# Running the token layers of the first image pair beside the last finish of the scan layers

## The chip, the cores and the metric

The kernel runs on one core of one Trainium2 chip. The metric is the device time of one launch in microseconds. Three runs of the kernel before gave 11881.9 us in the median, from 11853.94 to 11897.37. PE is the matrix engine (PEld its weight loads), DVE the vector engine, ACT the scalar engine, POOL the GpSimd engine, and SP the engine whose queue (SPq) issues the DMAs.

## The reference

Four images of 64x64 positions with 96 channels go through four layers, each with a residual addition.

```python
# layers 0 and 1: group norm, then a selective scan in four directions
x = x + conv_ref(_gn(x), ...)     # projection, 3x3 depthwise conv, SiLU, four scans of 16 states,
                                  # sum of the directions, layer norm, times silu(z), projection
# layers 2 and 3, on tokens: attention without a softmax, then a quantised MLP
t = t + attn_ref(_ln_t(t), ...)   # y = (q k^T) v * scale per head, then a projection
t = t + ffn_ref(_ln_t(t), ...)    # relu(W1 x + b1) in fp8, W2 h + b2
```

The end of a scan layer (the sum of the four directions, the layer norm, the gate `silu(z)`, the projection and the residual) is called the finish here. Layers 2 and 3 are the token layers. Every image is independent of the others in all four layers.

## The kernel before, in words

The images are worked on in pairs. Layers 0 and 1 make four phases: layer 0 on pair 0 and pair 1, then layer 1 on pair 0 and pair 1. Each phase has a preparation (`prepare`), the scan itself (`scan_phase`, whose order is written by hand) and a finish. `Scans.run` runs the preparation of a phase with the finish of the phase before it beside it: both are Python generators, and a number called `beside` says how many finish steps are taken for each preparation step. After the fourth scan, `run` makes one more turn with nothing to prepare, in which the finish of layer 1, pair 1 runs alone. Its result goes to `x2[1]`; the result for pair 0, `x2[0]`, was written a whole phase earlier.

`finish` works in four quarters (L603 to L619 bring one quarter into the layout of tokens, with a matmul by permutations for each direction and a matmul of `ud_f`, and ACT copies of the result) and each quarter in two slices (`finish_slice`: statistics L642, reciprocal root `neg_rsqrt` L115 to L119, normalisation L652 to L657, the gate L669 and L672 with SiLU, product L676, turn back L683, projection L694, residual L696, store L702). A quarter yields 52 times, so the finish has 208 steps.

Then `token_layers` runs. Its pools are opened when the scans' pools are closed. It loads and quantises the weights (L744 to L755, 17 small DMAs on SP, the mask among them), and takes the pairs in turn. For a pair, two generators `image(b)` are stepped in turn: load `t` (L887), for each of two layers `attention` and then the MLP, and store. In both parts the image is cut into eight chunks of 512 tokens, and `side_by_side` keeps two chunks of an image going. So four chains, two for each image, are interleaved. An image has 136 steps: 35 for an attention and 33 for an MLP, twice.

Each chunk begins with a layer norm: a matmul with a matrix of 1/96 gives the mean in a PSUM bank (`mu`, L784), DVE subtracts (L786), ACT squares (L793), a second matmul gives the variance in a second bank (`var`, L797), and `neg_rsqrt` takes Ln (L115), Exp (L116) and Square (L117) on ACT and two DVE operations (L118, L119). L118 reads `var` again, so that bank is held through Ln, Exp and Square. The first chunk of every sweep preloads the activation table that holds both Ln and Exp (L795, 16 times in all). In an MLP three matmuls (L866) are cast by ACT into `h16` (L869), DVE adds and clips (L870) and casts to fp8 (L875), and three matmuls (L878) give `o`.

[...] In the token layers, pool `tp_a` has four for `mu`, `var`, `o` and the small products of the attention, `tp_h` two and `tp_kv` two. In the last finish, the pools `p_c`, `p_d` (for the preparation) and `p_f` (two banks for the finish) are open. Outside of the hand-ordered parts, the framework orders the instructions of each engine out of the program's order and its own idea of what is ready; every engine then runs its own list strictly in order.

Of the kernel before, what the change touches and what calls it, by code (L numbers as in the profile page):

```python
# [9 lines left out]
F32 = mybir.dt.float32  # L10
F16 = mybir.dt.float16
# [4 lines left out]
PSUM = bass.MemoryType.PSUM  # L16
# [3 lines left out]
NP = B // 2  # L20
HW = 64
L = HW * HW
C = 96
# [6 lines left out]
TC = 512  # L30
# [12 lines left out]
NF = HID // 128  # L43
# [69 lines left out]
def neg_rsqrt(nc, cst, var, ln, r, sq):  # L113

    nc.scalar.activation(ln, var, AF.Ln, bias=cst.eps[: var.shape[0]])  # L115
    nc.scalar.activation(r, ln, AF.Exp, scale=-0.5)  # L116
    nc.scalar.activation(sq, r, AF.Square, scale=SQRT_HALF)  # L117
    nc.vector.scalar_tensor_tensor(sq, var, EPS, sq, ALU.add, ALU.mult)  # L118
    nc.vector.scalar_tensor_tensor(r, sq, 1.5, r, ALU.subtract, ALU.mult)  # L119
# [11 lines left out]
class Scans:  # L131
# [11 lines left out]
    def bank(self):  # L143
        return self.p_c.tile([128, TC], F32, name="c")
# [563 lines left out]
    def run(self, phases):  # L708


        for p in range(len(phases) + 1):
            with self.tc.tile_pool(name="p_c", bufs=2, space=PSUM) as self.p_c, self.tc.tile_pool(
                name="p_d", bufs=2, space=PSUM
            ) as self.p_d, self.tc.tile_pool(name="p_f", bufs=2, space=PSUM) as self.p_f:
                end = self.finish(phases[p - 1]) if p > 0 else iter(())
                due = 0.0
                if p < len(phases):
                    for _ in self.prepare(phases[p]):
                        due += phases[p].beside
                        while due >= 1.0:  # L720
                            next(end, None)
                            due -= 1.0
                for _ in end:
                    pass
            if p < len(phases):
                self.scan_phase(phases[p])


@with_exitstack
def token_layers(ctx: ExitStack, tc, cst, a, layers, x_in, x_out):  # L730

    nc = tc.nc
    wp = ctx.enter_context(tc.tile_pool(name="tw", bufs=1))
# [1 line left out]
    raw_p = ctx.enter_context(tc.tile_pool(name="traw", bufs=2))  # L735
    big = ctx.enter_context(tc.tile_pool(name="tbig", bufs=2))
    cp = ctx.enter_context(tc.tile_pool(name="tchunk", bufs=4))
    p_a = ctx.enter_context(tc.tile_pool(name="tp_a", bufs=4, space=PSUM))
    p_h = ctx.enter_context(tc.tile_pool(name="tp_h", bufs=2, space=PSUM))
    p_kv = ctx.enter_context(tc.tile_pool(name="tp_kv", bufs=2, space=PSUM))  # L740

# [29 lines left out]
    def side_by_side(parts, width):  # L771

        parts, active = iter(parts), []
        while True:
            if len(active) < width:
                active += [p for p in (next(parts, None),) if p is not None]
            if not active:
                return
            active = [p for p in active if next(p, p) is not p]
            yield  # L780

    def layernorm(t, cut, out, first, **quant):
        mu = p_a.tile([128, TC], F32, name="pa")
        nc.tensor.matmul(mu[:C], cst.mean_c, t[:, cut], start=True, stop=True)  # L784
        tcn = cp.tile([C, TC], F32, name="tcn")
        nc.vector.tensor_tensor(tcn, mu[:C], t[:, cut], ALU.subtract)  # L786
        yield
        sq = cp.tile([C, TC], F32, name="sq")
        with ExitStack() as order:
            if first:  # L790

                order.enter_context(tc.manual_schedule(engines={mybir.EngineType.Activation}))
            nc.scalar.activation(sq, tcn, AF.Square)  # L793
            if first:
                nc.scalar.preload_act_table_set(LN_EXP)  # L795
        var = p_a.tile([128, TC], F32, name="pa")
        nc.tensor.matmul(var[:C], cst.mean_c, sq, start=True, stop=True)  # L797
        yield
        ln = cp.tile([C, TC], F32, name="ln")
        r = cp.tile([C, TC], F32, name="r")  # L800
        neg_rsqrt(nc, cst, var[:C], ln, r, sq)
        yield
        nc.vector.tensor_tensor(out, tcn, r, ALU.mult, **quant)

# [27 lines left out]
    def attention(t, w):  # L832

        tn = big.tile([C + 1, L], F32, name="tn")
        nc.gpsimd.memset(tn[C : C + 1, :], 1.0)  # L835
        vk_ps = p_kv.tile([C, C], F32, name="vk_ps")
        yield from side_by_side((keys_values(t, tn, vk_ps, w, c) for c in range(NC)), 2)

        vk = cp.tile([C, C], F32, name="vk", bufs=2)
        nc.vector.tensor_tensor(vk, vk_ps, cst.mask, ALU.mult)  # L840
        m_ps = p_a.tile([128, TC], F32, name="pa")[:C, :C]
        nc.tensor.matmul(m_ps, vk, w["ff"], start=True, stop=True)
        m1 = cp.tile([C, C], F32, name="m1", bufs=2)
        nc.vector.tensor_copy(m1, m_ps)
        yield
        m_ps = p_a.tile([128, TC], F32, name="pa")[: C + 1, :C]
        nc.tensor.matmul(m_ps, w["q_t"], m1, start=True, stop=True)
        m2 = cp.tile([C + 1, C], F32, name="m2", bufs=2)
        nc.vector.tensor_copy(m2, m_ps)
        nc.vector.tensor_tensor(m2[C : C + 1], m2[C : C + 1], w["bff"][C : C + 1], ALU.add)  # L850
        yield
        for c in range(NC):
            cut = slice(c * TC, (c + 1) * TC)
            o = p_a.tile([128, TC], F32, name="pa")
            nc.tensor.matmul(o[:C], m2, tn[:, cut], start=True, stop=True)  # L855
            nc.vector.tensor_tensor(t[:, cut], t[:, cut], o[:C], ALU.add)
            yield

    def ffn_chunk(t, w, c):
        cut = slice(c * TC, (c + 1) * TC)  # L860
        xq = cp.tile([C, TC], FP8, name="xq")
        yield from layernorm(t, cut, xq, c == 0, saturate=False)
        h16 = cp.tile([128, NF, TC], F16, name="h16")
        for f in range(NF):
            h_ps = p_h.tile([128, TC], F32, name="ph")
            nc.tensor.matmul(  # L866
                h_ps, w["w1"][:, f * 128 : (f + 1) * 128], xq, start=True, stop=True
            )
            nc.scalar.copy(h16[:, f], h_ps)  # L869
            nc.vector.tensor_scalar(  # L870
                h16[:, f], h16[:, f], w["b1"][:, f : f + 1], 0.0, ALU.add, ALU.max
            )
            yield
        hq = cp.tile([128, NF, TC], FP8, name="hq")
        nc.vector.tensor_copy(hq, h16, saturate=False)  # L875
        o = p_a.tile([128, TC], F32, name="pa")
        for f in range(NF):
            nc.tensor.matmul(o[:C], w["w2"][:, f], hq[:, f], start=f == 0, stop=f == NF - 1)  # L878
        yield
        o16 = cp.tile([C, TC], F16, name="o16")  # L880
        nc.scalar.copy(o16, o[:C])
        nc.vector.tensor_scalar_add(o16, o16, w["b2"])
        nc.vector.tensor_tensor(t[:, cut], t[:, cut], o16, ALU.add)

    def image(b):
        t = big.tile([C, L], F32, name="t")
        nc.sync.dma_start(t.rearrange("c (a p) -> c a p", p=64), x_in[b // 2, :, :, b % 2])  # L887
        for pre in layers:
            yield from attention(t, ws[pre])
            yield from side_by_side((ffn_chunk(t, ws[pre], c) for c in range(NC)), 2)  # L890
        nc.sync.dma_start(x_out[b], t)

    for pair in range(NP):
        both = [image(2 * pair), image(2 * pair + 1)]
        while both:
            both = [i for i in both if next(i, i) is not i]


def body(tc, a, out):
    nc = tc.nc  # L900
    with ExitStack() as ctx:
        cst = Consts(nc, a)
        cst.shared(ctx.enter_context(tc.tile_pool(name="const", bufs=1)))
        dram = ctx.enter_context(tc.tile_pool(name="dram", bufs=1, space=DRAM))
        x1 = dram.tile([NP, C, HW, 2, 64], F32, name="x1")
        x2 = dram.tile([NP, C, HW, 2, 64], F32, name="x2")
        phases = [Phase("L0_", p, a["x"], x1) for p in range(NP)]
        phases += [Phase("L1_", p, x1, x2) for p in range(NP)]
        with ExitStack() as inner:
            Scans(tc, inner, cst, a).run(phases)  # L910
        token_layers(tc, cst, a, ["L2_", "L3_"], x2, out)


def constants():
# [83 lines left out]
```

## Time and profile before

| what | value |
|---|---|
| profiled execution, its own time | 11923.01 us |
| its span, first to last instruction | 11921.2 us (1.8 us lie outside) |
| median of the three runs | 11881.9 us |
| last scan instruction ends, last finish begins | about 10728 us from the span's start |
| last finish ends | about 11055 us |
| pair 0 in the token layers | 11055 to 11482 us, its loads first |
| pair 1 in the token layers | 11482 us to the end |
| busy: PE, DVE, ACT, POOL | 72%, 84%, 62%, 63% of the span |

The span is the time from the first to the last recorded instruction. Busy time of PE is the time in which at least one matmul is under way by the record, with the tail of each matmul in it, so a PE that works in short pieces looks busier than one that works without a break. In the list of stages, each row gives the length of the stretch, the busy time and the instruction count of each engine, the mean granted clock of PE as a share of full speed, the DMA share and the rate.

### The profile page before, as it was taken

The numbers are of one execution on the slowest core, as the hardware profiler recorded it, in microseconds if no ns is written. First come the engines' busy times: TensorE is split into PE (matmuls) and PEld (weight loads), VectorE is DVE, ScalarE is ACT, GpSimd is POOL, SyncE is SP. The second block draws the span as 40 slices with busy tenths as digits, with TensorE's granted clock in tenths as the row PEclk, the third lists the DMA queues.
The fourth block names the chain that finished last, engine by engine and source line by source line (L and its number), as shares of the span: only waits on it lengthen the run. The fifth ranks groups of instructions, "written<-read, shape, count | busy, mean of one in ns | idle before, by whom it ended". The sixth has DMA issues, their size and how long they took to land.

```text
span 11921.2 us, 337611 instructions
## 1 busy us (share of the span) xinstructions
PE 8549.8 (72%) x144992; PEld 4586.7 (38%) x144992; DVE 9991.8 (84%) x10247; ACT 7335.1 (62%) x12106; POOL 7480.2 (63%) x2316
## 2 busy tenths in 40 slices
PE   4557777765767777765767777766667777777777
PEld 1124444432334444442334444433234444444333
DVE  6679999977779999987769999986769999993667
ACT  4556666655556666655556666655557666662556
POOL 0169999961159999970149999980149999980000
PEclk8578999986679999986679999887578898998887
DMA  3677777765677777765777777765677777763110
GB/s 99 192 244 250 253 255 254 251 208 144 201 241 256 253 253 251 253 217 146 204 229 258 256 253 251 253 217 149 198 226 255 255 255 253 253 229 124 18 22 11
DMA packets 952266, 2501.22 MB, mean 210 GB/s; under 512 B 324494, under 2 KB 607220, under 8 KB 819316
## 3 DMA queue, kind: packets, MB, share of 16 engines
q1 hardware_dynamic: 950772, 2479.63, 63.0%
q8 instruction: 1142, 18.71, 0.7%
q14 instruction: 352, 2.88, 0.1%
HBM read 1965.42 MB, written 513.80 MB: 208 GB/s over the span
## 4 chain that ended last, share of the span: by engine, by line
DMA 57%; PE 12%; DVE 11%; SPq 10%; ACT 5%; issue 3%; POOL 2%; POOLq 0%; DVEq 0%; ACTq 0%
DMA h<-du 53%; SPq L408 9%; DVE xc L277 4%; PE f L603 2%; POOL parts L331 2%; PE d L317 1%; DVE dl L328 1%; PE f L683 1%; PE c L300 1%; DVE du_sb L327 1%; PE f L694 1%; DVE parts L332 1%; DMA yk<-y 1%; PE f L669 1%; PE f L612 1%
## 5 line engine op out<-in xcount | busy, mean ns | idle before, releaser
L418 POOL TENSOR_TENSOR h<-h,b 128x1536 f32<-128x1536 f32 x2048 | 7020.9, 3461 | 574.0 <-DMA h<-du 229.6
L435 DVE TENSOR_TENSOR_SCAN h<-a,carry,h 128x512 f32<-128x512 f32 x5376 | 6353.3, 1259 | 202.8 <-POOL h L418 199.4
L428 ACT ACTIVATE a<-a,a_col 128x512 f32<-128x512 f32 x6144 | 4038.5, 664 | 1888.6 <-PE a L424 1852.8
L453 PEld LDWEIGHTS y<-h,cw 128*32 128x32 f32 x131072 | 2785.0, 128 | 3534.2 <-issue 1369.4
L453 PE MATMUL y<-h,cw 128*32 128x48 f32 x131072 | 3658.4, 266 | 522.4 <-DVE h L435 205.3
L424 PE MATMUL a<-dlt,rep 72*128 72x512 bf16 x6144 | 2534.2, 422 | 1352.5 <-DVE h L435 1254.1
L331 POOL CAST parts<-dl 96x1024 bf16<-96x1024 f32 x256 | 431.2, 1688 | 2687.6 <-DVE dl L328 1979.4
L465 ACT COPY d<-y 128x384 f32<-128x384 f32 x2048 | 979.7, 478 | 467.7 <-PE y L453 414.9
L435 DVE TENSOR_TENSOR_SCAN h<-a,h 128x512 f32<-128x512 f32 x768 | 868.2, 1200 | 179.7 <-ACT a L428 113.4
L277 DVE SCALAR_TENSOR_TENSOR xc<-xp,conv_w,xc 96x512 f32<-96x512 f32 x1024 | 716.3, 760 | 154.2 <-ACT xc L275 110.0
L424 PEld LDWEIGHTS <-rep 72*128 72x128 bf16 x6144 | 487.5, 98 | 849.3 <-issue 613.9
L317 PE MATMUL d<-xd,dt_w 7*96 7x512 f32 x1024 | 532.0, 885 | 263.6 <-ACT dl L325 141.2
L835 POOL MEMSET tn<- 1x4096 f32 x8 | 27.8, 3506 | 861.5 <-PE pa L855 515.4
L300 PE MATMUL c<-xc,x_proj 96*103 96x512 f32 x512 | 442.0, 1002 | 115.7 <-ACT xp L261 54.6
L327 DVE TENSOR_TENSOR du_sb<-dl,xc 96x1024 f32<-96x1024 f32 x256 | 409.9, 1607 | 123.6 <-ACT dl L325 67.2
L603 PE MATMUL f<-yk,perm 128*128 128x384 f32 x1024 | 415.6, 549 | 106.4 <-DMA yk<-y 81.0
L325 ACT ACTIVATE dl<-d 96x1024 f32<-96x1024 f32 x256 | 257.7, 1018 | 348.6 <-DVE parts L332 259.2
L328 DVE TENSOR_TENSOR dl<-dl,parts 96x1024 f32<-96x1024 f32 x256 | 309.8, 1216 | 190.7 <-ACT parts L326 187.8
L332 DVE TENSOR_TENSOR parts<-dl,parts 96x1024 bf16<-96x1024 f32 x256 | 326.2, 1280 | 170.0 <-POOL parts L331 168.8
L317 PEld LDWEIGHTS d<-xd,dt_w 7*96 7x96 f32 x1024 | 160.0, 216 | 586.5 <-ACT xd L303 200.1
L258 PE MATMUL c<-rawi,in_ws 96*96 96x512 f32 x256 | 195.5, 874 | 241.3 <-ACT xp L261 101.6
L370 ACT ACTIVATE cw<-c,gmask 128x256 f32<-128x256 f32 x512 | 285.5, 569 | 129.3 <-DMA dlt<-delta 66.7
(119 smaller groups left out, 5764.0 us busy)
## 6 DMA issues: line engine op xcount, KB each, us to landing
h<-du SPq DMA_DIRECT2D x1024, 768.0 KB
h<-du SPq DMA_DIRECT2D x2048, 384.0 KB
du<-du_sb SPq DMA_DIRECT2D x512, 384.0 KB
delta<-parts SPq DMA_DIRECT2D x256, 576.0 KB
dlt<-delta SPq DMA_DIRECT2D x512, 288.0 KB
y<-d SPq DMA_DIRECT2D x2048, 48.0 KB
yk<-y SPq DMA_DIRECT2D x256, 384.0 KB
ud<-xu SPq DMA_DIRECT2D x128, 192.0 KB
```

The lines of the kernel that those rows point to most:

```text
L277: nc.vector.scalar_tensor_tensor(rows(acc), src, w, rows(acc), ALU.mult, ALU.add)
L300: nc.tensor.matmul(rows(ps[:XD2]), xp[:, k, h], u[:, h], start=h == 0, stop=h == 1)
L317: nc.tensor.matmul(ps[:, m], dt_w[part, k, m * C : (m + 1) * C], xd[part], start=True, stop=True)
L331: nc.gpsimd.tensor_copy(parts[:, 1], delta)
L408: self.nc.sync.dma_start(u.h[32 * first : 32 * (first + quarters), e : e + n].rearrange("p e t -> p (e t)"), source.rearrange("a g e t -> ...
L418: self.nc.gpsimd.tensor_tensor(h, h, b, ALU.mult)
L424: self.nc.tensor.matmul(u.a[n], self.cst.rep[:, h], u.dl[:, e], start=True, stop=True)
L428: self.nc.scalar.activation(u.a[n], u.a[n], AF.Exp, scale=u.ph.a_col[:, at : at + 1])
L435: self.nc.vector.tensor_tensor_scan(u.h[:, n], u.a.pop(n), u.h[:, n], 0.0 if u.c == 0 else u.ph.carry[:, at : at + 1], ALU.mult, ALU.add,)
L453: self.nc.tensor.matmul(view(u.y[32 * j : 32 * j + 32], l2 * EB, (8 * EB, 4), (1, EB)), u.ph.cw[u.c][:, l1, 8 * j + l2], view(u.h, 64 * l1 ...
L465: self.nc.scalar.copy(u.d[:, :, :, l1], u.y[:, : 32 * EB].rearrange("p (t h x) -> p t h x", t=4, h=2))
L603: nc.tensor.matmul(ps[:, : 4 * C].rearrange("p (w v e) -> p w v e", w=4, v=nv), cst.perm[:, k], view(t, off, (sw if k < 2 else -sw, 4), (1 ...
```

## The change

The extra turn of `run` is taken out. `token_layers` is called while the scans' pools for kept tensors and constants are still open, and gets the finish of the last phase as a generator. It steps both images of pair 0 once for every two steps of the finish, until the finish has ended; then it goes on with the images alone. While the finish lasts, the pool `tp_a` has two banks, since the finish's `p_f` takes two; after it, a pool `tp_b` of two banks is opened in their place, and the tiles are taken from the two pools in turn. To fit into the memory, `neg_rsqrt` writes its logarithm into `r` in place of a tile `ln`, and `h16` has three buffers in place of four.

```diff
-        for p in range(len(phases) + 1):
+        for p in range(len(phases)):
...
-                if p < len(phases):
-                    for _ in self.prepare(phases[p]):
-                        due += phases[p].beside
-                        while due >= 1.0:
-                            next(end, None)
-                            due -= 1.0
+                for _ in self.prepare(phases[p]):
+                    due += phases[p].beside
+                    while due >= 1.0:
+                        next(end, None)
+                        due -= 1.0
...
-def token_layers(ctx: ExitStack, tc, cst, a, layers, x_in, x_out):
+def token_layers(ctx: ExitStack, tc, cst, a, layers, x_in, x_out, scans, last):
...
-    p_a = ctx.enter_context(tc.tile_pool(name="tp_a", bufs=4, space=PSUM))
+    spaces = [ctx.enter_context(tc.tile_pool(name="tp_a", bufs=2, space=PSUM))]
+    taken = [0]
+
+    def bank():
+        taken[0] += 1
+        return spaces[taken[0] % len(spaces)].tile([128, TC], F32, name="pa")
+
...
-        mu = p_a.tile([128, TC], F32, name="pa")
+        mu = bank()
...
-        ln = cp.tile([C, TC], F32, name="ln")
         r = cp.tile([C, TC], F32, name="r")
-        neg_rsqrt(nc, cst, var[:C], ln, r, sq)
+        neg_rsqrt(nc, cst, var[:C], r, r, sq)
...
-        h16 = cp.tile([128, NF, TC], F16, name="h16")
+        h16 = cp.tile([128, NF, TC], F16, name="h16", bufs=3)
...
+    def step(images):
+        return [i for i in images if next(i, i) is not i]
+
+    both = [image(0), image(1)]
+    with tc.tile_pool(name="p_f", bufs=2, space=PSUM) as scans.p_f:
+        end = scans.finish(last)
+        while next(end, end) is not end:
+            next(end, None)
+            both = step(both)
+    spaces.append(ctx.enter_context(tc.tile_pool(name="tp_b", bufs=2, space=PSUM)))
     for pair in range(NP):
-        both = [image(2 * pair), image(2 * pair + 1)]
         while both:
-            both = [i for i in both if next(i, i) is not i]
+            both = step(both)
+        if pair + 1 < NP:
+            both = [image(2 * pair + 2), image(2 * pair + 3)]
...
-            Scans(tc, inner, cst, a).run(phases)
-        token_layers(tc, cst, a, ["L2_", "L3_"], x2, out)
+            scans = Scans(tc, inner, cst, a)
+            scans.run(phases)
+            token_layers(tc, cst, a, ["L2_", "L3_"], x2, out, scans, phases[-1])
```

The other places that took a tile from `p_a` (the variance, the small products of the attention, `o`) call `bank()` in the same way.

More of the change, by code (lines that the diff above doesn't have):

```diff
@@ L716, in run @@
                 due = 0.0
-                if p < len(phases):
-                    for _ in self.prepare(phases[p]):
-                        due += phases[p].beside
-                        while due >= 1.0:
-                            next(end, None)
-                            due -= 1.0
+                for _ in self.prepare(phases[p]):
[3 more added lines that the diff above has]
+                        due -= 1.0
                 for _ in end:
                     pass
-            if p < len(phases):
-                self.scan_phase(phases[p])
+            self.scan_phase(phases[p])
 @with_exitstack
-def token_layers(ctx: ExitStack, tc, cst, a, layers, x_in, x_out):
+def token_layers(ctx: ExitStack, tc, cst, a, layers, x_in, x_out, scans, last):
     nc = tc.nc
@@ L795, in layernorm @@
                 nc.scalar.preload_act_table_set(LN_EXP)
-        var = p_a.tile([128, TC], F32, name="pa")
+        var = bank()
         nc.tensor.matmul(var[:C], cst.mean_c, sq, start=True, stop=True)
         yield
-        ln = cp.tile([C, TC], F32, name="ln")
         r = cp.tile([C, TC], F32, name="r")
-        neg_rsqrt(nc, cst, var[:C], ln, r, sq)
+        neg_rsqrt(nc, cst, var[:C], r, r, sq)
         yield
@@ L840, in attention @@
         nc.vector.tensor_tensor(vk, vk_ps, cst.mask, ALU.mult)
-        m_ps = p_a.tile([128, TC], F32, name="pa")[:C, :C]
+        m_ps = bank()[:C, :C]
         nc.tensor.matmul(m_ps, vk, w["ff"], start=True, stop=True)
@@ L845, in attention @@
         yield
-        m_ps = p_a.tile([128, TC], F32, name="pa")[: C + 1, :C]
+        m_ps = bank()[: C + 1, :C]
         nc.tensor.matmul(m_ps, w["q_t"], m1, start=True, stop=True)
@@ L853, in attention @@
             cut = slice(c * TC, (c + 1) * TC)
-            o = p_a.tile([128, TC], F32, name="pa")
+            o = bank()
             nc.tensor.matmul(o[:C], m2, tn[:, cut], start=True, stop=True)
@@ L875, in ffn_chunk @@
         nc.vector.tensor_copy(hq, h16, saturate=False)
-        o = p_a.tile([128, TC], F32, name="pa")
+        o = bank()
         for f in range(NF):
```

## The prediction

> **What bounds the kernel now.** I first read the page's slices, to see where the scans end.
>
> ```profile
> POOL 0169999961159999970149999980149999980000
> PEclk8578999986679999986679999887578898998887
> ```
>
> POOL works only in the scans, so the last four slices of 298 us, which end with a POOL digit of 0, are the last finish and the token layers: 10728 us to the end, 1193 us of the span. Nothing ahead of that is touched by the change. Then I cut this part, and for comparison two preparations, into stages.
>
> ```profile
> 0.00:710.00 710.00, 327.87 (x470) 99.14 (x471) 446.50 (x509) 327.46 (x359) 104.38 (x68) 0.65 0.58 161
> 2601.00:3427.00 826.00, 532.04 (x1430) 255.16 (x1431) 551.04 (x773) 420.48 (x511) 109.36 (x64) 0.65 0.64 183
> 10728.00:11055.00 327.00, 233.02 (x960) 161.87 (x960) 104.30 (x272) 85.23 (x144) 0.00 (x0) 0.84 0.37 117
> 11055.00:11085.00 30.00, 2.17 (x3) 0.40 (x2) 6.18 (x14) 1.91 (x2) 6.95 (x2) 0.53 0.93 141
> 11085.00:11171.00 86.00, 81.29 (x359) 49.24 (x360) 53.41 (x87) 50.97 (x96) 0.78 (x1) 0.96 0.00 1
> 11171.00:11282.00 111.00, 75.62 (x161) 23.68 (x160) 84.53 (x159) 72.98 (x129) 6.18 (x2) 0.69 0.00 0
> 11282.00:11369.00 87.00, 81.84 (x363) 49.38 (x362) 55.96 (x91) 53.19 (x99) 1.12 (x1) 0.98 0.00 1
> 11369.00:11482.00 113.00, 75.25 (x160) 23.19 (x158) 85.75 (x161) 73.56 (x130) 5.84 (x2) 0.70 0.01 3
> ```
>
> After the length come PE, PEld, DVE, ACT, POOL busy, the granted PE clock, DMA share and GB/s. Rows 3 to 8 are the finish, the loads of the token layers, and attention, MLP, attention, MLP of pair 0: 754 us in all. The finish has DVE busy for 32% and ACT for 26% of its 327 us; it is a chain. The attention has PE busy for 94%. In the MLP no engine is above 76%. The waits of the finish say what kind of chain it is.
>
> ```profile
> ACT s L619 <- PE f L612: 115.7, 30, 13.8
> ...
> PE f L603 <- DMA yk<-y: 39.7, 10, 15.0
> ```
>
> ACT waits 115.7 us for PE's rearranging matmuls, and PE 39.7 us for the transfers that bring each quarter. This idle time is what other work could use. How much PE really needs is seen in single runs of matmuls.
>
> ```profile
> 10881.00 5.46 PE L669 MATMUL f<-in_w,xm 96*128 96x192 f32 x16 [6.51 <-DVE xm L661]
> ...
> 10897.71 2.75 PE L603 MATMUL f<-yk,perm 128*128 128x384 f32 x8
> ```
>
> After an idle 6.51 us, 16 matmuls of 192 columns take 5.46 us (0.34 each; granted clock of 10881 to 10886.5: 0.52); in a run without a break, 8 of twice the columns take 2.75 us, the same 0.34 each. So part of PE's busy time is slow clock.
>
> **What moves.** The finish has 208 steps, two to a turn, so 104 turns; an image has 136. Attention, MLP and attention of pair 0 fill turns 1 to 103; the second MLP follows with four banks. So the 754 us become: a start, a mixed stage of finish and three quarters of pair 0, and an MLP of 113 us as in the last row. Pair 1 (loads 29 us, then 410) is unchanged but for `h16`.
>
> **Work in the mixed stage**, rows 3, 5, 6, 7. DVE: 104 + 53 + 85 + 56 = 298 us. ACT: 85 + 51 + 73 + 53 = 262 us, before reloads. PE: 233 + 81 + 76 + 82 = 472 us as recorded; with each row times its granted clock, 233 x 0.84 + 81 x 0.96 + 76 x 0.69 + 82 x 0.98 = 196 + 78 + 52 + 80 = 406 us at full clock. The Trainium skill ("TensorE: Matmul & The Clock Gate", Part 1: The HAM clock gate) says that PE drops to half clock after a window of about 3.4 us idle and returns after a busy one. The two rows above agree, 0.52 after 6.5 us. Which sum holds depends on gaps: if the mixed stream keeps the old clocks, PE needs 472, and the stage at 80% busy lasts 590; if it is dense enough to stay fast, 406 and 508. I take 406, since the attention, the denser row, has 0.96 to 0.98.
>
> **The activation tables speak against the change.**
>
> ```profile
> L115 ACT ACT_TABLE_LOAD x8 | 10.3, 1283 | 0.1
> L116 ACT ACT_TABLE_LOAD x8 | 10.3, 1283 | 0.1
> L672 ACT ACT_TABLE_LOAD x8 | 10.3, 1283 | 0.1
> ```
>
> These are the loads of the finish alone: each of its eight slices loads a table for Ln, one for Exp, one for SiLU. The token layers load 16 times in 128 layer norms, by the preload, which is kept since nothing else comes between. In the mixed stage SiLU comes between. By the order of steps, SiLU falls in turns 12-13, 20-22, 38-39, 46-48, 64-65, 72-74, 90-91, 98-100 and the preloads in turns 2, 37, 70, 105. So per image 4 of the first 8 layer norms, all 8 of the MLP and 7 of the second attention run without the joint table: 38 for both images, up to two loads each, 76 x 1.283 = 97 us; one each, 49 us, if the order puts two Ln and two Exp together. SiLU itself may need one more load per slice, 10 us. I take 90 us of the range 49 to 107, near the upper end, since a load stood between every Ln and Exp of the finish: ACT 352 us. The skill ("ScalarE: Activation LUTs", What ACT_TABLE_LOAD costs, and the table sets after it) would count differently: 2.66 us for a switch with its drain, but one load for Ln followed by Exp. The trace shows two loads for such a pair, and an activation 1.29 us after the load began (10778.62, then 10779.91). With its price and the trace's count, 76 loads are 202 us, ACT needs about 460 and would be the bound at 575 for 80%. I use the row.
>
> **Banks.** A chain's variance bank, from the timeline:
>
> ```profile
> 11140.00 1.02 PE L797 MATMUL pa<-sq,mean_c 96*96 96x512 f32 x2
> 11141.12 0.67 ACT L115 ACTIVATE ln<-pa,eps 96x512 f32<-96x512 f32 x1
> ...
> 11143.14 0.69 DVE L118 SCALAR_TENSOR_TENSOR sq<-pa,sq 96x512 f32<-96x512 f32 x1 [0.53 <-ACT sq L117]
> ```
>
> 3.8 us from matmul to release here, 5.3 at 11132.9; a mean bank takes 1.7 to 3.3. So 7 us per layer norm now; with two reloads and about 4 us of queueing behind the finish (one 2.75 us run on PE, one 1.76 us operation on DVE), 13.5. The stage has 48 layer norms and 48 products held about 2 us: (48 x 13.5 + 96) / 2 = 372 us for two banks, below PE's time. At 7 us it would be 216, at 20 us 528.
>
> **Length of the mixed stage.** Best case: PE at the 94% of the attention, 406 / 0.94 = 432. Worst: nothing overlaps and the reloads are all on the path, 327 + 86 + 111 + 87 + 97 = 708. PE and ACT at 406 and 352, with banks at 372, are close to each other, so none fills up; I take PE at 80%, between the MLP's and the attention's fullest engine (76% and 94%): 508 us.
>
> **Start.** Finish and token loads now share SP's queue: 17 small DMAs and two of `t`, issued in 0.3 to 0.6 us each, about 8 us, with a wait for quantisation that took 10 us in the trace if the order keeps it in front. Queued behind it are the finish's loads, and PE waits for these. `t` took 11.5 us to land. The finish's first matmul came 11 us after 10728; I take 26 us for first work, between 11 and the 30 of row 4.
>
> **Small edits.** Ln in place writes on the same engine in the same order: nothing, cover is the in-order ACT queue. `h16` with three buffers makes the fourth chain wait for the first cast to fp8; there are 16 groups of four chains in both pairs, 27.5 us each, 12 casts there. It may also let the first chain finish earlier, so -1 to +2 us per group, taken as +0.5: 8 us. If the casts of the other three did not cover the wait, it is the 2 us. Two pools in turn, two banks each: nothing, as four banks in order; bounded by one late bank per sweep, +-5 us. The wait of `tp_b` for `p_f` lies at turn 105, when the finish ends by count; if the finish lags, all token work behind it on PE waits with it.
>
> **Sum.** 26 + 508 + 113 + 8 = 655 in place of 754: 99 us less. Against the profiled execution, 11921.2 + 1.8 - 99 = 11824; that execution was 41 us above the median, so the median goes from 11882 to 11783.
>
> **A check.** Preparation alone takes 710 us, with a finish beside it 826 (rows 1 and 2): 116 more for 327 of finish, 65% hidden. Here 99 of 327 is 30%, less because the preparation leaves PE at 46% and the token layers do not.
>
> **Rivals.** *As well hidden as beside the preparation* (0.2): 65% of 327 is 211; with the reloads partly on the path some 170 are left, 11712. For it: the row; against: PE would have to be at over 90%. *Eaten up* (0.22): PE keeps its clocks, 472 / 0.8 = 590, or ACT pays the page's price, 575: 754 - 26 - 590 - 113 - 8 = 17 us gained, 11865. *Slower* (0.13): the two banks. In the variance hold lie Ln and Exp, and a chain that finds the other chain's Ln and Exp with two loads ahead of it waits 2 x (1.28 + 0.65) = 3.9 us each time, besides the finish's runs. The gain is gone when the stage reaches 607 us, that is a hold of (1214 - 96) / 48 = 23 us per layer norm; at 28 us it is 720 and the kernel comes to 11995. For it: PE, ACT and DVE keep order, so holds add up; against: two to three such waits more per layer norm than I count are needed. *The token work does not start beside the finish*, for lack of memory or a dependence through `x2`, is a case of no change; `x2[0]` was complete a phase before, so I give it 0.02 and put it into "eaten up".
>
> **How the numbers follow.** 0.45 for the forecast, whose own range is 11725 to 11825 (PE at 90% to 74%). A difference of 0.5%, 59 us, is about what a measurement of this kernel can tell from no change. Faster by more: forecast (nearly all) and well hidden, 0.63; within: eaten up and the forecast's edge, 0.24; slower: 0.13. The range, 11705 to 11900, takes in the well hidden case and the eaten-up case and leaves most of the slower one out.
>
> **What would show it.** Right: the end of the finish some 500 us after the scans, PE about 80% busy with a clock over 0.9 in that stage, 50 to 80 loads for L115 and L116 beyond the eight each, the second MLP near 113 us. Wrong: PE waiting for `pa` banks (released by L118 or L786), a clock of 0.8, many more loads, or MLP stages of pair 1 longer than 111 us by more than 8.

## The result, and the profile after

| | before | after |
|---|---|---|
| median | 11889.47 us (20 runs) | 11846.71 us (20 runs) |
| ratio after to before | | 0.9968, interval 0.9957 to 0.9978 |
| profiled span | 11921.2 us | 11867.0 us |
| last scan matmul to last residual addition of the finish | 332 us | 605 us, with three quarters of pair 0 beside it |
| last scan matmul to the store of pair 0 | 758 us | 720 us |
| store of pair 0 to the end | 439 us | 443 us |

The gain is 0.32% by the ratio, some 38 us (the medians lie 43 apart), where 99 were forecast. In the profiled runs the 54 us between the spans are 35 behind the last scan matmul and 19 ahead of it, in code that the change doesn't touch. So the comparisons below count from the last scan matmul, at 10724.2 us before and 10704.8 us after. The slices of the page after:

```profile
POOL 0169999961159999970149999980139999990000
PEclk8579999986679999986579998996669999998877
```

The slices with a POOL digit of 0 are still four, but the clock digits in them are 8, 8, 7, 7, where they were 8, 8, 8, 7: no slice of the mixed stage shows a clock of 0.9 or more. The stages of the trace after, cut at the first token matmul, the end of the finish, the store of pair 0 and the first matmul of pair 1:

```profile
10705.00:10749.00 44.00, 16.96 (x64) 11.12 (x65) 2.29 (x13) 2.31 (x5) 6.95 (x2) 0.69 0.82 166
10749.00:11310.00 561.00, 448.56 (x1779) 272.26 (x1780) 297.68 (x608) 370.78 (x548) 10.12 (x3) 0.86 0.21 63
11310.00:11424.00 114.00, 76.03 (x159) 24.06 (x157) 84.94 (x161) 73.16 (x130) 3.81 (x2) 0.66 0.01 4
11424.00:11450.00 26.00, 3.80 (x4) 0.79 (x4) 1.05 (x2) 1.91 (x2) 0.00 (x0) 0.54 1.07 226
11450.00:11867.00 417.00, 310.61 (x1037) 145.18 (x1036) 278.33 (x495) 250.01 (x454) 6.96 (x2) 0.80 0.03 8
```

The start takes 44 us before token work begins and the mixed stage 561; 26 and 508 were forecast. The second MLP takes 114 us; 113 were forecast. In the mixed stage PE is busy for 80%, ACT for 66%, DVE for 53%. The finish's own waits have shrunk. ACT's wait for the rearranging matmuls is 53.9 us in the mixed stage (41 more lie in the start, so 95 in all), where 115.7 were in the finish alone. And the group of these matmuls says in its last column that transfers cost 0.9 us of PE's time here. Before, it was 39.7 us with the first wait of 15.0; the first wait here, 26.1 us, lies in the start.

```profile
ACT s L619 <- PE f L612: 53.9, 19, 12.7
```

```profile
L603 PE MATMUL f<-yk,perm 128*128 128x384 f32 x224 | 86.7, 514 | 0.9 <-DMA yk<-y 0.9
```

What came beside them stands among the longest waits of the mixed stage, as microseconds in all, number and longest:

```profile
DVE sq L118 <- ACT sq L117: 112.2, 40, 9.1
...
PE pa L788 <- DVE sq L118: 19.7, 8, 6.4
...
PE pa L801 <- DVE sq L118: 11.7, 6, 4.2
```

and in the groups of ACT from the last scan matmul to the end of the finish:

```profile
L115 ACT ACT_TABLE_LOAD x43 | 55.2, 1283 | 0.8
L116 ACT ACT_TABLE_LOAD x43 | 55.2, 1283 | 0.8
...
L672 ACT ACT_TABLE_LOAD x20 | 25.7, 1283 | 0.3
```

Where the finish alone had 24 loads there are 106, besides the preloads. DVE stands for 112 us in front of L118, the step of a layer norm that releases the variance bank, because ACT is late with the square ahead of it, and PE waits 31 us for banks which that step releases. One layer norm on ACT shows how:

```profile
11138.50 1.28 ACT L115 ACT_TABLE_LOAD   x1
11139.79 0.68 ACT L115 ACTIVATE r<-pa,eps 96x512 f32<-96x512 f32 x1
11141.07 0.68 ACT L115 ACTIVATE r<-pa,eps 96x512 f32<-96x512 f32 x1 [0.59 <-PE pa L801]
11141.72 0.48 ACT L824 COPY kv<-ph 128x384 f32<-128x384 f32 x1
11142.21 1.28 ACT L116 ACT_TABLE_LOAD   x1
11143.51 0.63 ACT L116 ACTIVATE r<-r 96x512 f32<-96x512 f32 x1
```

From the first load to the Exp of the first chain 5.0 us pass. Two loads are only half of it; the rest is that Ln of the second chain, which waits for its own matmul, and a copy stand between. Matched one by one in the trace, the 48 variance banks of the mixed stage are held 8.74 us on average, the 48 of the same stages before 5.42.

### The profile page after: what moved, and what is told of

It is laid out like the page before. It is cut to its first block, busy times and chain, and to the rows that moved or that the text cites. A ratio compares the mean times of both kernels' runs of the same rounds, so it can differ in the third digit from the quotient of the medians.

```text
span 11867.0 us, 337689 instructions
## 1 busy us (share of the span) xinstructions
PE 8543.5 (72%) x144992; PEld 4588.6 (39%) x144992; DVE 9985.5 (84%) x10247; ACT 7439.0 (63%) x12188; POOL 7479.5 (63%) x2316
## 4 chain that ended last, share of the span: by engine, by line
DMA 57%; PE 11%; DVE 11%; SPq 10%; ACT 6%; issue 3%; POOL 2%; POOLq 0%; DVEq 0%; ACTq 0%
DMA h<-du 53%; SPq L408 9%; DVE xc L277 5%; PE f L603 2%; POOL parts L331 2%; DVE dl L328 1%; PE f L683 1%; DVE du_sb L327 1%; PE d L317 1%; PE f L694 1%; DVE parts L332 1%; PE c L300 1%; DMA yk<-y 1%; PE f L612 1%; PE ph L816 1%
```

## The experiments

Three theories: **reloads** (the table loads stand in the chain and reach the end), **banks** (two are too few), **order** (the two streams stop each other on engines that work in order). "Stage" is the time from the last scan matmul to the last residual addition of the finish, in the profiled run: 605 us for the changed kernel. The expectations count 601 us, from a start some 3 us later. Ratios are to the kernel before, with 95% intervals.

| run | loads in the stage | stage, us | ratio |
|---|---|---|---|
| changed kernel | 112 | 605 | 0.9968 (0.9957 to 0.9978) |
| no_silu | 6 | 489 | 0.9873 (0.9858 to 0.9888) |
| preload_after_gate | 64 | 552 | 0.9923 (0.9906 to 0.9940) |
| early_release | 119 | 611 | 0.9979 (0.9971 to 0.9986) |
| before_two_banks | 24 | 332 | 1.0039 (1.0025 to 1.0053) |
| before_small_edits | 24 | 335 | 0.9991 (0.9982 to 1.0001) |
| gate_by_exp | 6 | 517 | 0.9887 (0.9873 to 0.9902) |
| loads_in_norm | 6 | 487 | 0.9885 (0.9872 to 0.9898) |
| loads_in_finish | 102 | 523 | 0.9901 (0.9884 to 0.9918) |
| norm_loads_two | 96 | 551 | 0.9929 (0.9913 to 0.9945) |
| norm_loads_one | 54 | 519 | 0.9890 (0.9870 to 0.9910) |
| no_silu_early | 6 | 501 | 0.9890 (0.9870 to 0.9909) |
| gate_loads | 42 | 503 | 0.9870 (0.9849 to 0.9891) |
| all_loads | 109 | 557 | 0.9937 (0.9922 to 0.9951) |
| late_root | 91 | 550 | 0.9938 (0.9925 to 0.9951) |

The two runs on the kernel before, before_two_banks and before_small_edits, have the finish alone in their stage. The runs whose names begin with no_silu, norm_loads or loads_in, and gate_loads and all_loads, leave out the SiLU of the last finish; the others compute everything. Profiled stages are single executions.

The framework orders the instructions anew for every program, so no run changes the loads alone. Loads aside, ACT has 441 instructions in the stage and DVE 621. In the longest sequence common to both programs, the changed kernel shares 365 and 525 of them with no_silu, 410 and 577 with preload_after_gate, 342 and 483 with all_loads.

**Without SiLU.**

```diff
-                ..., ps[:, : 2 * E], AF.Silu
+                ..., ps[:, : 2 * E], AF.Identity if self.last else AF.Silu
```

> Leaves out the SiLU of the last finish (Identity in its place, the same size on ACT), so that nothing drives the joint Ln and Exp table out. Three theories for the 67 us by which the mixed stage and its start came out longer than forecast (601 us from the end of the scan to the end of the last finish, where 534 were forecast). Reloads: the table loads stand in the chain of every layer norm; then about 100 loads less (16 preloads stay), the variance hold falls from 8.7 us to about 6, and the 601 us become about 530, ratio to the kernel before about 0.991. Banks: two banks are the limit; the shorter hold helps only in part, about 580 us, 0.995. Order: the two streams stop each other on engines that work in order, whatever the tables do; 590 us or more, 0.996.

The stage fell to 489 us, more than even the reload theory expected. Its mixed part:

```profile
10747.00:11192.00 445.00, 405.85 (x1779) 251.38 (x1778) 295.11 (x608) 232.65 (x442) 10.23 (x3) 0.95 0.26 78
```

PE is busy for 91% at a clock of 0.95, against 80% at 0.86 above; of the wait of DVE for ACT's last square 20 us are left:

```profile
DVE sq L118 <- ACT sq L117: 20.3, 20, 4.9
```

SiLU with its table loads is the cause of the missing gain, in the sense that without it the gain is all there. How the loads do it, and how much is due to the other order, was left to tell.

**The joint table again after the gate.** Behind the fourth SiLU of a slice, held to that place:

```diff
+                if joint:
+                    nc.scalar.preload_act_table_set(LN_EXP)
```

> Computes everything; after the fourth SiLU of each slice of the last finish the joint table is loaded again, held to that place on ACT. Loads for Ln and Exp only where a layer norm falls between the SiLUs of one slice: some 20 in place of 86, plus 8 preloads, plus the SiLU's own 20; about 60 less, 75 us of ACT. Reloads: the 601 us fall to about 550, ratio about 0.993. Banks or order: 590 us or more, 0.996 to 0.997.

Not quite half of the extra loads went (64 are left in place of 112), and 53 of the 116 us: 1.1 us for each of 48 loads. The reload theory had about 550. This is the run nearest to the changed kernel in its order, so its 1.1 us is the best price here for a load where the two streams drive out each other's table.

**Banks, three times.** In the changed kernel and in the one without SiLU, DVE copies the variance out:

```diff
+        if len(spaces) == 1:
+            held = cp.tile([C, TC], F32, name="held", bufs=2)
+            nc.vector.tensor_copy(held, var)
+            var = held
```

> In the mixed stage alone DVE copies the variance out of PSUM at once (48 copies of 0.7 us, 33 us of DVE, which is busy 53% there), and Ln and the last step read the copy; the table loads stay as they are. The bank is then held about 2 us in place of 8.7. Banks: PE's 31 us of waiting for L118 go and more with it, 601 to about 550 us, ratio 0.993. Reloads: the chain is longer by the copy, 600 to 615 us, 0.997 to 0.998. Order: within 10 us of 601.

> Leaves out the SiLU of the last finish and copies the variance out of its bank at once: two banks are then held about 2 us each and no load is in the way. What is left of the price of two banks once the loads are gone: with banks as a limit 489 goes to 460 us or less, ratio 0.985; without, 480 to 500, 0.987 to 0.988, as the copies lengthen the chain by 0.7 us each.

611 us in place of 605 (with seven loads more), and 501 in place of 489: releasing the bank early helps in neither. In the first the variance bank is held 3.3 us on average in place of 8.74, and PE's wait for its release is gone, but another has come in front of the same matmul:

```profile
PE pa L801 <- ACT sq L797: 29.0, 13, 5.9
```

The third is the kernel before with `bufs=2` for `tp_a`.

> The kernel before with two banks in place of four in the token layers, nothing else: the price of two banks with no reloads and no finish beside. By the trace of before a layer norm holds its two banks for 2.15 and 5.42 us; 128 of them and 136 products of about 2 us are 1240 bank-us, 620 us for two banks against 836 us of token time now. Banks: +100 us or more, ratio 1.008 or more. Reloads or order: +10 to +40 us, 1.001 to 1.003.

The ratio of 1.0039 is 46 us for all four images, between the two expectations: in the profile 20 us for pair 0 and 21 for pair 1. Two banks cost something where all four chains run alone, some 15 us for three quarters of a pair, but they are not what holds the mixed stage.

**The edits that make room.**

```diff
-        h16 = cp.tile([128, NF, TC], F16, name="h16")
+        h16 = cp.tile([128, NF, TC], F16, name="h16", bufs=3)
```

and the logarithm in `r`.

> The kernel before with the two edits that make room in memory and nothing else: h16 with three buffers, the logarithm written into r. The prediction took +8 us for both pairs, between -16 and +32: ratio 1.0007, between 0.9987 and 1.0027. No theory of the mixed stage needs it elsewhere.

0.9991 with an interval that touches 1: no cost, perhaps a gain of some 10 us.

**Loads in place of SiLU.** With Identity in the gate, loads were put in by hand, to separate ACT's time from the place of the loads. First in the layer norms, each behind `with tc.manual_schedule(...)` at the head of a block with Ln or Exp:

> Leaves out the SiLU of the last finish as before, and puts two table loads of the joint set into every layer norm of the mixed stage, ahead of Ln and ahead of Exp: 96 loads, 123 us of ACT, all in the chain of the token layers and none in the finish. If the place of the loads decides (between a layer norm's variance and its release), the stage goes from 489 us back to about 590, ratio 0.996. If only the ACT time counts, the same 590 here and with the loads in the finish. If neither, because it was the order that the framework chose around SiLU, about 500, 0.988.

```profile
L800 ACT ACT_TABLE_LOAD x16 | 20.5, 1283 | 0.3
```

Only the 16 preloads are in the trace; the loads put in by hand are missing. The run tells nothing of loads and is a repetition of the run without SiLU: PE, DVE and ACT have the same instructions in the same order in the stage. The two stages took 487 and 489 us, the two ratios are 0.9885 and 0.9873; that is how far a repetition can lie off. Then behind the finish's copies, which worked:

> Leaves out the SiLU of the last finish, and puts one table load of the joint set behind each ACT operation that empties a bank of the finish (32 of the layout, 32 of the gate, 32 of the turn back): 96 loads, 123 us of ACT, none between Ln and Exp of a token layer norm. If the place in the layer norm decides: 500 to 530 us for start and mixed stage, ratio 0.988 to 0.991. If ACT's time counts wherever it lies: about 590, 0.996.

```profile
L155 ACT ACT_TABLE_LOAD x96 | 123.2, 1283 | 1.7
```

123 us more of ACT cost 34 us of the stage, 0.35 us for each load. So ACT's time alone is not it. Then in the layer norms, behind the square and behind Ln:

```diff
+            nc.scalar.activation(r, var[:C], AF.Ln, bias=cst.eps[:C])
+            nc.scalar.preload_act_table_set(LN_EXP)
```

> Leaves out the SiLU of the last finish. The run before with loads in the layer norms carried only 16 loads, since a load that finds its set in place at the head of such a block was dropped; here they stand behind the square and behind Ln, as the loads of the finish stood behind its copies: 90 loads more than without SiLU, 115 us of ACT, all between a layer norm's first square and its Exp. Place in the layer norm decides: stage and start go from 489 us to 570 to 600, ratio to the kernel before 0.995 to 0.997. Only ACT's time counts: as with the loads in the finish, 523 us, 0.990 to 0.991. The order chosen around SiLU is the cost, not the loads: under 500, 0.988.

> The same with one load for each layer norm, between Ln and Exp: 48 loads, 62 us of ACT. If each load in the chain costs about the same, the stage goes half of the way of the run with two: 530 to 545 us, ratio 0.991 to 0.993. If the first load is covered and only the second reaches the end: 500, 0.988 to 0.989.

90 loads cost 62 us and 48 cost 30, about 0.65 us each. They cost nearly twice what they cost behind the finish's copies, so the place matters, but no expected number was met: 551 lies between the 523 of ACT's time and the 570 to 600 of the place, and 519 between the 500 and the 530 to 545.

**What the rest is.** Two runs more put loads at the finish's Ln, Exp and gate, alone and together with loads in chunks 2 to 7 of the layer norms:

> Leaves out the SiLU of the last finish and puts 36 loads of the joint set where the changed kernel has its loads in the finish: ahead of Ln once for a quarter, and in each slice between Ln and Exp, ahead of the gate and between its first operations; none in the layer norms. If loads in the gate's chain reach the end in full, 36 x 1.28 = 46 us: start and stage 489 to 535 us, ratio to the kernel before 0.991. If they cost what the loads behind the finish's copies cost, 0.35 us each: 13 us, 502, 0.989.

> The same 36 loads in the finish, and 67 in the layer norms of chunks 2 to 7 (behind the square and behind Ln): 103 loads more than without SiLU, about as many and at about the places as in the changed kernel, which has 106 more. If the loads by themselves are the whole cost: 590 to 610 us for start and stage, ratio 0.996 to 0.997. If part of the 116 us is the order that the framework chooses with SiLU in the program: 540 to 565 us, 0.992 to 0.994.

36 loads in the gate's chain cost 14 us by the profile, 0.4 each; the ratio, 0.9870, shows no cost. All 103 together cost 68 us, 557 in place of 605, with about the count and the places of the changed kernel. Its mixed part, and DVE's wait for ACT's last square, which here has two lines: L835 in the 36 layer norms with loads, L118 in the other 12:

```profile
10770.00:11285.00 515.00, 442.71 (x1784) 267.54 (x1782) 297.06 (x609) 361.48 (x546) 10.76 (x4) 0.88 0.22 68
```

```profile
DVE sq L835 <- ACT sq L834: 68.7, 30, 6.3
...
DVE sq L118 <- ACT sq L117: 12.8, 6, 5.0
```

ACT is busy for 361 us as against 371, the variance banks are held 8.23 us as against 8.74, and DVE waits 81.5 us for that square as against 112. So the loads put in by hand bring back most of what the changed kernel shows, but only 68 of the 116 us. A load over a table that is already in place costs ACT as much as one that changes the table: every load lasts 1.283 us in both kernels, and ACT's next instruction starts 1.29 us after the load began (the median of each). So that is not the difference. The remaining 48 us are not explained by the number of loads and their rough place. The order is another in the two kernels, as counted above; whether it is that, stays open. The last run moves the end of the reciprocal root one step back in the program:

```diff
             nc.scalar.activation(sq, r, AF.Square, scale=SQRT_HALF)
+            yield
             nc.vector.scalar_tensor_tensor(sq, var[:C], EPS, sq, ALU.add, ALU.mult)
```

> Computes everything; table loads as in the changed kernel. In the mixed stage the two DVE operations that end the reciprocal root come one step later in the program, behind the other chains' and the finish's work of that step, so that DVE need not stand in front of them while ACT loads tables (112 us of DVE's idle time in the changed kernel, 20 without SiLU, 13 with the same loads put in by hand). The chains have 12 steps more before the finish is done, so I compare the time from the last scan matmul to the store of pair 0, 720 us in the changed kernel. If the order on DVE is the 48 us that the loads in number and place did not explain: 670 to 690 us, ratio to the kernel before 0.992 to 0.994. If it is not: 715 or more, since the variance banks are held longer, 0.996 to 0.998.

The 13 us in its expectation is L118 of all_loads alone; with L835 it is 81.5. Pair 0 is stored after 680 us in place of 720, with all of the computation, and the ratio is 0.9938, both as expected if the order on DVE were the cause. But the run doesn't show that: it also has 21 fewer loads (91), which at 0.65 to 1.1 us are 14 to 23 us of the 40, and DVE still waits at the very step that was moved.

```profile
DVE sq L809 <- ACT sq L807: 86.9, 33, 6.6
```

By this estimate the other order in itself would be worth some 17 to 26 us. That the 48 us of all_loads are the order is argued and not shown. That they are DVE standing at this one step is not borne out: the wait there is 31 us shorter in all_loads than in the changed kernel, and in late_root 87 us of it are left.

**A version that beats both.** In the last finish SiLU is made of functions that the joint table holds:

```diff
         nc.vector.tensor_tensor(s, s, z, ALU.mult)
+        if self.last:
+            nc.scalar.activation(z, z, AF.Exp, scale=-1.0)
+            nc.scalar.activation(z, z, AF.Ln, bias=self.ones)
+            nc.scalar.activation(z, z, AF.Exp, scale=-1.0)
+            nc.vector.tensor_tensor(s, s, z, ALU.mult)
```

> Computes everything. In the last finish SiLU is made of functions of the joint table: z times exp(-ln(1 + exp(-z))), three more ACT operations of 128x1536 and one more DVE product of 128x1536 for each of the eight slices, in place of SiLU; so no table changes in the mixed stage. Without SiLU the stage and its start took 489 us. The four added operations are about 1.4 us each on ACT and 1.76 on DVE, 6 us in the chain of each slice, 48 us in all, of which the token work should cover three quarters. Theory that the reloads are on the path: 500 us, ratio to the kernel before 0.988 to 0.990. If the reloads only cost what ACT has to do (the theory that ACT's work counts), 34 us of ACT come back in place of 136: about 520 us, 0.990. Banks: 560 or more.

```profile
10702.00:11176.00 474.00, 412.22 (x1784) 253.70 (x1783) 309.25 (x617) 265.83 (x467) 13.93 (x4) 0.94 0.24 74
```

0.9887, 1.13% faster than the kernel before, with no loads in the stage but the six preloads. The added operations, 36 us of ACT and 14 of DVE, cost 28 us against no SiLU at all, more than the 11 expected, and save 88 against the changed kernel. 517 us is nearer to the 520 of the theory that only ACT's work counts than to the 500 of the other, so this run does not part the two; loads_in_finish does, where 123 us of ACT cost 34.

## Why the prediction was wrong

**The step that failed is "Length of the mixed stage".** It took the reloads as 90 us of ACT's work, which would lie beside PE's since ACT's 352 us were below PE's 406, and put PE at 80% of its full-clock work. The runs show SiLU with its reloads as a term of its own: 605 - 489 = 116 us for 106 loads, 1.09 us each if all is put down to them; preload_after_gate gives 1.1. Loads put in by hand bring back 68 of the 116; from where the other 48 come, beyond SiLU being in the program, stays open. Without SiLU the stage is 489 us where the prediction, counted from the last scan matmul, had 538. So everything else in that sum was 49 us too long, and the reloads, at nothing beyond the 80%, 116 us too short; the difference, 67 us, is the missing gain and a little more. That the 49 us stand against the 116 is luck: without them the forecast would have been further off.

**The counts in it were right.** 76 loads for Ln and Exp and 8 for SiLU were forecast beyond the finish's own 24, at most, and 70 and 12 came, 82 of 84. ACT was forecast with 352 us and had 371, DVE 298 and 298. PE's work at full clock, busy time times granted clock, was 406 in the sum and is 449 x 0.86 = 386 in the mixed stage after, the same 406 x 0.95 = 386 without SiLU (17 x 0.69 = 12 us more lie in the start of both). But 386 of 561 is 69%, and 386 of 445 is 87%. That PE is recorded as busy for 80% of the stage, the number of the forecast, is chance: the forecast meant 80% at full clock.

**The clock.** The prediction took the faster clock because the mixture would be denser. It is 0.95 without SiLU and its loads and 0.86 with them, the mean that the four stages before had (406 of 472). The rival's "PE keeps its clocks" came near with its number, 590 us for a stage that took 561, but without SiLU and its loads the clock rose, so it is no cause beside them.

**The tables.** The Trainium skill ("ScalarE: Activation LUTs", What ACT_TABLE_LOAD costs, and the table sets after it) gives one load to Ln followed by Exp; the changed kernel shows 43 and 43. Its rule to batch by set is what these runs support most: with all of the computation kept, a gate made of functions of one set is worth 88 us here (gate_by_exp). Its 2.66 us for a switch would have led near the measured time by a wrong way: no run shows more than 1.1 us of the stage for a load, and ACT's next instruction starts 1.29 us after a load began.

**Banks.** A hold of 13.5 us per layer norm was estimated, 2.35 + 8.74 = 11.1 measured. The rival "slower", which hung on it, did not come. PE does wait 31 us for banks, as the prediction's sign of being wrong had it, but early_release took that wait away and the stage was no shorter: the bank isn't the limit.

**Start.** The finish's first matmul came 26 us after the last scan matmul (10730.9); the forecast counted its 26 from 4 us later, so that was nearly right. Token work began 18 us after it:

```profile
10729.89 14.19 SPq L890 DMA_DIRECT2D t<-x  x2
```

the two issues of `t` held SP's queue for 14 us, and the finish's next loads stood behind them. The forecast priced them at 1.2 us; the trace before could have warned of it, where the two issues of `t` for pair 1, at 11489.3, take 10.7 us.

**The rest.** The second MLP was 113 in the forecast and 114 after. The small edits, +8 us in the sum, measured 0.9991, between its bounds but not above 1. The case "eaten up", 11865 us, is the nearest to the measured 11847.

## What to carry to other kernels

When two streams are laid side by side, list for each engine not only its busy time but the state that each stream needs there, here the activation table. A switch of state is not work of that engine that hides below another's bound: it falls between two steps of a chain, in an order fixed beforehand. Here between 0.35 and 1.1 us of each load of 1.28 us reached the end. Make both streams use one table, or price each switch at up to its own length.

## What the runs showed of the hardware

A table load of 1.283 us cost the stage 0.35 us behind a copy that empties a bank, 0.4 us in the gate's chain, about 0.65 us in a layer norm, and 1.1 us where two streams drive out each other's table (48 loads, 53 us, in preload_after_gate; all 106 with SiLU, 116 us). In the last figure some part may be the order of the instructions, which changed too. Taking SiLU and its loads away also gave PE a faster clock: 0.86 to 0.95 with the same matmuls in 445 us in place of 561.
